# Two batch pairs through layer 3 with seven quarter products, and layer 0 of the first pair on two engines

## The chip, the core and the metric

The kernel runs on one core of a Trainium2 chip. The metric is the device time of one launch in microseconds. The core has a matrix engine (PE, which multiplies a stationary 128x128 operand with up to 512 moving columns into PSUM), a vector engine (DVE), an activation engine (ACT), GpSimd (POOL) and a queue engine (SP). All of them run their own instruction streams in order and meet through semaphores. Transfers between HBM and the on-chip memory are issued here by SP (loads of the adjacency matrix A) and by POOL (nearly everything else).

## What is computed

`x` is 8 x 2048 x 64, `adj` is a dense-stored 2048 x 2048 f32 matrix. Four layers follow each other; each adds its result to x and normalises over the 64 channels. Cut to what matters:

```python
# layer 0: Chebyshev stack, node-wise weights
x_g = [x, A @ x, 2 * A @ (A @ x) - x]                    # two products with A
out = einsum('bnki,nkio->bno', x_g, einsum('nd,dkio->nkio', embedding, weight)) + b
# layer 1: attention masked by adj > 0.5, softmax over nodes, elu
# layer 2: one product with A + I
agg = einsum('ij,bjh->bih', adj + eye, x @ W.T + b) / deg
# layer 3: three steps, one product with A each
for _ in range(3):
    effects = einsum('nm,bmd->bnd', adj, v)
    h = relu(concatenate([v, effects]) @ W1.T + b1)
    v = h @ W2.T + b2
x = layernorm(x + v)
```

## The kernel before

**Tiling.** The batch of 8 is worked on as four pairs; two batches of 64 channels fill the 128 rows of the array. A node vector of a pair is a [128, 16, 128] tile: nodes in 16 groups of 128, and 128 channels. `SX[p]` holds pair p, `SA`, `SB` and `SH` are further slots of that form. One product with A (`sweep`, L1040) runs over four column chunks of 512 nodes; each chunk accumulates 16 matmuls of 128x128 by 128x512, that is 64 per product. A comes as tiles [128, 2, 512] of 512 KB, two matmuls' worth, through a ring of seven buffers (`a_ring`, L219), which `fetch` (L223) fills in the order of `order_of_a`. All products are in full f32. In the profile each such matmul has two records.

**Stages.** `sweeps` (L1108) runs the products: the first product of pairs 0 and 1 on shared A tiles, then each pair's second product with the first one of a later pair, then for each pair in turn its layer 2 and its three steps of layer 3. In a step, `U = h W` is held for all nodes; the product's result goes through `h_evict` (L917, relu on ACT into `SH`), and `u_chunk` (L990) multiplies that chunk by a 128x128 block and writes the next U. `last_chunk` (L1010) and `store` (L1030) end a pair. The product of a step starts with a seed, one more 128x512 matmul per chunk for the part of W1 that acts on v (L1048).

Layer 0's node-wise weights are applied in `second_pass` (L553): for each tile of 128 nodes, two halves of 8 terms are multiplied into a PSUM buffer of two banks. `add_terms` (L590) drains a half by 8 ACT instructions, scaling by the embedding, into an SBUF tile `terms`; after the second half DVE adds up the 16 terms as a tree (L612). When all four buffers of that ring are taken, DVE drains with multiply-adds directly (L601). The PSUM buffers come from `pp_ring` (two of them), which also serves all transposes and small products. `po_ring` (one buffer) belongs to the attention product.

Layer 1 (`layer1`, L635, to `finish`, L828): `layer1` transposes x and makes the scores' two vectors; `scores` (L676) finds each row's greatest score on DVE with 32 instructions; `weights` (L773) makes the 16 x 2 blocks of attention weights, two DVE additions and two ACT passes each; PE multiplies them with x (L810); `finish` divides and normalises. When a pair is done, `at["x2", p]` is set, on which its layer 2 waits. The scores of a pair wait for those of the pair before. The mask by rows comes from `rows_of_adj` (L400), which loads adj row-wise, 1 MB per tile, at due times 115 + 13 t.

**What sets the order.** A planner, executed while the program is built, holds an estimated time for each engine and a set of generators ("threads"). Each thread says on which engine it wants to go on and after what; the thread that can begin first is emitted next, so each engine's stream is a merged, fixed order. The product sweeps have the lowest rank and fill PE when nothing else is ready. PE work that waits for something is planned with 2.5 us of slack. `tails` (L937) emits the small PE work behind each chunk in the order of the evictions.

Of the kernel before, what the change touches and what calls it, by code (L numbers as in the profile page):

```python
# [9 lines left out]
F32 = mybir.dt.float32  # L10
# [125 lines left out]
def resnorm_d4_kernel(  # L136
# [57 lines left out]
    def cols(c):  # L194
        return slice(c * CW, (c + 1) * CW)
# [24 lines left out]
    a_tiles = {}  # L220
    order_of_a = []

    def fetch(n):  # L223
        c, q, plus = order_of_a[n]
        t, k = a_ring.take([P, 2, CW], "a")
        freed = a_ring.t
        nc.sync.dma_start(
            t,
            a_plus_i[q]
            if plus and c == q // 2  # L230
            else adj_t[q * 2 * P : (q + 1) * 2 * P, cols(c)].rearrange("(t p) n -> p t n", p=P),
        )
        a_tiles[n] = (t, k)
        at["a", n] = plan.run("SP", 1.4, freed) + 3.5

# [91 lines left out]

    a_plus_i = [dram.tile([P, 2, CW], F32, name=f"a_plus_i{q}") for q in range(AQ)]

    y1_cols = [dram.tile([P, N], F32, name=f"y1_cols{p}") for p in range(NPAIR)]  # L330


# [67 lines left out]
    def rows_of_adj():  # L400


        for t in range(NT):
            yield "SP", [115.0 + 13.0 * t, bc_ring]
            an, k = bc_ring.take([P, 2, HALF], "an")
            an = an.rearrange("p a b -> p (a b)")
            nc.sync.dma_start(an, adj[t * P : (t + 1) * P, :])
            done = plan.run("SP", 2.8, bc_ring.t, 115.0 + 13.0 * t) + 9.0
            plan.start(1, row_tile(t, an, k, done))

    def row_tile(t, an, k, done):
# [141 lines left out]
    def second_pass():  # L553

        for n in range(NPAIR * NCH):
            yield "PE", [("y2", n + 1), ("xg", n + 1)]
            p, c, y2T, ky, got = queue[n]
            xg, kx = stacked[n]
            left = [TPC]
            for j in range(TPC):  # L560
                t = c * TPC + j
                cs = slice(j * P, (j + 1) * P)
                for h in range(2):
                    hs = slice(h * CW, (h + 1) * CW)
                    if h == 0 or pp_ring.ready() > plan.free["PE"]:
                        yield "PE", [("xg", n + 1), got, pp_ring]
                    if h == 0:


                        terms = None  # L570
                        if e_ring.ready() < NEVER:
                            terms = e_ring.take([P, D0, P], "terms")
                    yp, k = pp_ring.take([P, 2, CW], "yp")

                    for k2 in (h, 1 - h):
                        for e in range(2):
                            rows = slice(e * C, (e + 1) * C) if k2 else slice(0, P)
                            nc.tensor.matmul(  # L578
                                yp[:, e, :],
                                lhsT=y2T[rows, cs] if k2 else xg[:, e, cs],  # L580
                                rhs=(wk2 if k2 else w01)[rows, hs],
                                start=(k2 == h),
                                stop=(k2 != h),
                            )
                    t_pe = plan.run("PE", 2.8, got)
                    plan.start((2, 2, 1, 1)[p], add_terms(p, c, t, h, yp, k, terms, t_pe, left))
            yt_ring.give(ky, t_pe)
            xg_ring.give(kx, t_pe)

    def add_terms(p, c, t, h, yp, k, terms, t_pe, left):  # L590
        eng = "ACT" if terms else "DVE"
        yield eng, [t_pe]
        v = SX[p][:, t, :]
        for d in range(8):
            dd = h * 8 + d
            term = yp[:, :, d * C : (d + 1) * C]
            weight = emb_sb[:, t, dd : dd + 1]
            if terms:
                nc.scalar.activation(batches(terms[0][:, dd, :]), term, AF.Copy, scale=weight)  # L599
            else:  # L600
                nc.vector.scalar_tensor_tensor(  # L601
                    batches(v), term, weight, batches(v), ALU.mult, ALU.add
                )
        done = plan.run(eng, 8 * (0.25 if eng == "ACT" else 0.265), t_pe)
        pp_ring.give(k, done)
        if h == 0:
            return
        if terms:
            yield "DVE", [done]
            for half in (8, 4, 2):  # L610
                a, b = (terms[0][:, i * half : (i + 1) * half, :] for i in range(2))
                nc.vector.tensor_tensor(a, a, b, ALU.add)  # L612
            for d in range(2):
                nc.vector.tensor_tensor(v, v, terms[0][:, d, :], ALU.add)
            done = plan.run("DVE", 2.5, done)
            e_ring.give(terms[1], done)
        left[0] -= 1
        if left[0] == 0:
            plan.start(2, first_norm(p, c, plan.free["DVE"] + plan.LAG))
# [282 lines left out]

    def after_l2(p):
        return SB if p == 0 else SX[p - 1]

    def z_evict(p, c, pa, ka, done):
        yield "ACT", [done, yt_ring]
        z, kz = yt_ring.take([P, CW], "z")  # L910
        nc.scalar.copy(z, pa)
        done = plan.run("ACT", act(CW), done)
        acc_ring.give(ka, done)
        queue2.append(lambda: layer2_tail(p, c, z, kz, done))
        at["q2", len(queue2)] = done

    def h_evict(p, s, c, pa, ka, done):  # L917
        yield "ACT", [done]
        nc.scalar.activation(  # L919
            SH[:, tiles(c), :],  # L920
            pa.rearrange("p (t n) -> p t n", n=P),
            AF.Relu,
            bias=b31b if s == 0 else b31n,
        )
        done = plan.run("ACT", act(CW), done)
        acc_ring.give(ka, done)
        at["h", p, s, c] = done
        if s < 2:
            dst = SX[p] if s == 0 else SA
            queue2.append(lambda: u_chunk(p, c, ge, dst, ceb, s + 1, done))  # L930
        else:
            queue2.append(lambda: last_chunk(p, c, done))
        at["q2", len(queue2)] = done
# [33 lines left out]
    def start_chunk(p, c, v, done):  # L967

        done = yield from layer_norm(v, CW, done, True)
        if c == 0:  # L970
            v00 = tiny([P, P], "v00", 1)
            nc.vector.tensor_copy(v00, v[:, 0, :])
            nc.vector.tensor_copy(
                v00[0:1, :].rearrange("p (e c) -> p e c", c=C),
                ivc.unsqueeze(1).to_broadcast([1, 2, C]),
            )
            done = plan.run("DVE", dve(P, 2), done)
        yield "PE", [done, pp_ring]
        pt, k = pp_ring.take([P, TPC, P], "ps_vT")
        for j in range(TPC):  # L980
            nc.tensor.transpose(pt[:, j, :], v00 if c + j == 0 else v[:, j, :], ident)
        done = plan.run("PE", tr(TPC), done)
        eng = yield EITHER, [done]
        copy(eng, SH[:, tiles(c), :], pt)
        done = plan.run(eng, cost(eng, CW), done)
        pp_ring.give(k, done)
        at["h", p, -1, c] = done
        yield from u_chunk(p, c, w31e, SA, None, 0, done)

    def u_chunk(p, c, w, dst, bias, s, done):  # L990
        yield "PE", [done, pp_ring]
        pu, k = pp_ring.take([P, TPC, P], "ps_u")
        for j in range(TPC):
            nc.tensor.matmul(  # L994
                pu[:, j, :], lhsT=SH[:, c * TPC + j, :], rhs=w, start=True, stop=True
            )
        done = plan.run("PE", mm(P, TPC), done)
        if bias is None:
# [11 lines left out]
    def last_chunk(p, c, done):  # L1010
        yield "PE", [done, pp_ring]
        pv, k = pp_ring.take([P, TPC, P], "ps_v")
        for j in range(TPC):
            nc.tensor.matmul(  # L1014
                pv[:, j, :], lhsT=SH[:, c * TPC + j, :], rhs=w32c, start=True, stop=True
            )
        done = plan.run("PE", mm(P, TPC), done)
        at["spent", p, c] = done
# [62 lines left out]
    def refill():  # L1081
        while ahead[0] < len(order_of_a) and a_ring.ready() < NEVER:
# [2 lines left out]
            fetch(ahead[0])  # L1085
            ahead[0] += 1

    def first_product(p):
        return product(SX[p], lambda c, *a: y1_chunk(p, c, *a))

# [3 lines left out]
        )  # L1094

    def layer2_product(p):
        return product(SX[p], lambda c, *a: z_evict(p, c, *a), need=lambda q: [("x2", p)])

    def layer3_product(p, s):
        return product(  # L1100
            SX[p] if s == 1 else SA,
            lambda c, *a: h_evict(p, s, c, *a),
            need=lambda q: [("u", p, s, q)],
            before=lambda c: [("h", p, s - 1, c)],
# [3 lines left out]
    def sweeps():  # L1108

        order_of_a.extend((c, q, False) for _ in range(NPAIR) for c, q in sweep_of_a)  # L1110
        for p in range(NPAIR):
            for s in range(4):
                order_of_a.extend((c, q, s == 0) for c, q in sweep_of_a)
        refill()
        yield from sweep(first_product(0), first_product(1), masks=True)
        for p in range(NPAIR):
# [1 line left out]
            if 0 < p < NPAIR - 1:  # L1118
                products.append(first_product(p + 1))
            yield from sweep(*products)  # L1120
        for p in range(NPAIR):
            yield from sweep(layer2_product(p))
            for s in range(3):
                yield from sweep(layer3_product(p, s))


    ctx.enter_context(tc.manual_schedule())
# [47 lines left out]
```

## Time and profile before

| | |
|---|---|
| median of 3 runs | 2182.61 us (2180.09 to 2184.45) |
| profiled execution | 2179.89 us |
| its span, first to last instruction | 2178.1 us |
| granted PE clock | 0.993 |
| busy: PE, DVE, ACT, POOL | 2116.7, 1424.8, 973.0, 194.6 us |
| moved | 504.26 MB, mean 232 GB/s |
| A tiles loaded | 672 of 512 KB, 5.2 us to landing |
| layer 0 of pair 0 on PE | 151 to 311 us |
| first scores (pair 0) | 377.5 us |
| first layer-2 matmul of pair 2 | 1649.2 us |
| layer 1 of pair 3 done | 1707.6 us |
| last product ends, last store is issued | 2165.5, 2171.9 us |

A row of a timeline reads: start, duration, engine, line, operation, output<-inputs, shape, count; in brackets the idle time before it and what ended it. "xN" merges N instructions of a kind. The costliest groups of PE and ACT in layer 0, with busy time, mean ns of one and idle time before:

```profile
L578 PE MATMUL yp<-SH,xgT 128*128 128x512 f32 x512 | 249.9, 611 | 5.3 <-issue 2.1
L599 ACT ACTIVATE terms<-yp,emb_sb 128x128 f32<-128x128 f32 x928 | 251.8, 396 | 104.9 <-PE yp L578 104.8
```

Matmuls and ACT instructions are pipelined, so their mean durations overlap; a rate is read from a run of them, not from the mean.

### The profile page before, as it was taken

To read this page: it belongs to the slowest core of one execution; us is meant where nothing else is said; L and a number is where in the kernel's file an instruction comes from. 1 tells how busy PE (TensorE), PEld (TensorE's weight loads), DVE (VectorE), ACT (ScalarE), POOL (GpSimd) and SP (SyncE) were. 2 spreads that over 40 slices of the span, in tenths; PEclk is the share of its full clock that TensorE was granted. 3 is DMA by queue.
4 is the path that set the end of the run, shared out by engine and by line. 5 is a ranking of instruction groups with operands and counts; after the bars stand their busy time and mean duration, and the time that the engine had idled before them with its cause. 6 is when DMAs were issued, how large, how long until landed. Compare 5 with 4: busy or idle time off the path is not lost. (4 is left out here: it accounts for less than half of the span.)

```text
span 2178.1 us, 19094 instructions
## 1 busy us (share of the span) xinstructions
PE 2116.7 (97%) x6421; PEld 934.0 (43%) x6421; DVE 1424.8 (65%) x1823; ACT 973.0 (45%) x1761; POOL 194.6 (9%) x342
## 2 busy tenths in 40 slices
PE   8999999999999999999999999999999999999997
PEld 3444444433443333335443444444444544444443
DVE  2215554999789999989998989989797400121002
ACT  0016664467776555675724757417476200111001
POOL 2210000110011010000001011011010000000000
PEclk9999999999999999999999999999999999999999
DMA  9798764564344473347689778788787777887785
GB/s 312 270 323 297 241 201 146 165 208 123 113 159 122 132 245 110 121 129 258 214 304 345 237 274 297 255 307 292 241 270 226 247 263 269 282 289 247 265 277 182
DMA packets 228453, 504.26 MB, mean 232 GB/s; under 512 B 20530, under 2 KB 28850, under 8 KB 224242
## 3 DMA queue, kind: packets, MB, share of 16 engines
q1 hardware_dynamic: 189378, 372.79, 51.0%
q0 software_dynamic: 34752, 128.14, 17.4%
q10 hardware_dynamic: 4224, 2.10, 0.4%
q8 instruction: 51, 0.84, 0.2%
q14 instruction: 48, 0.39, 0.1%
HBM read 471.31 MB, written 29.56 MB: 230 GB/s over the span
## 5 line engine op out<-in xcount | busy, mean ns | idle before, releaser
L1059 PE MATMUL acc<-a,SX 128*128 128x512 f32 x1536 | 693.8, 597 | 9.4 <-DMA SX<-in_x 6.4
L1059 PE MATMUL acc<-a,SA 128*128 128x512 f32 x1280 | 575.0, 596 | 8.9 <-ACT SA L337 4.8
L1059 PEld LDWEIGHTS acc<-a,SX 128*128 128x128 f32 x1536 | 285.6, 191 | 350.7 <-issue 336.4
L1059 PEld LDWEIGHTS acc<-a,SA 128*128 128x128 f32 x1280 | 238.8, 191 | 293.9 <-issue 278.6
L792 ACT ACTIVATE e<-e,sv 128x1024 f32<-128x1024 f32 x256 | 280.9, 1153 | 108.8 <-DVE e L784 107.3
L706 DVE CUSTOM_DVE_ANT_0 junk<-s2b,mr 128x2048 bf16<-128x2048 f32 x128 | 292.8, 2287 | 24.3 <-DMA mr<-by_row 22.9
L800 ACT ACTIVATE e<-e 128x2048 f32<-128x2048 f32 x128 | 245.0, 1918 | 128.5 <-DVE e L797 128.0
L599 ACT ACTIVATE terms<-yp,emb_sb 128x128 f32<-128x128 f32 x928 | 251.8, 396 | 104.9 <-PE yp L578 104.8
L797 DVE TENSOR_TENSOR e<-e,mb 128x2048 f32<-128x2048 f32 x128 | 290.5, 2286 | 4.9 <-ACT e L792 4.7
L784 DVE TENSOR_TENSOR e<-s1b,mk 128x2048 f32<-128x2048 f32 x128 | 289.8, 2285 | 3.1 <-DMA mk<-by_col 3.1
L578 PE MATMUL yp<-SH,xgT 128*128 128x512 f32 x512 | 249.9, 611 | 5.3 <-issue 2.1
L810 PE MATMUL po<-e,SX 128*64 128x512 f32 x1024 | 236.4, 603 | 4.0 <-ACT e L800 4.0
L612 DVE TENSOR_TENSOR terms<-terms 128x1024 f32<-128x1024 f32 x174 | 135.7, 780 | 106.0 <-ACT terms L599 101.9
L578 PEld LDWEIGHTS yp<-SH,xgT 128*128 128x128 f32 x512 | 90.6, 190 | 149.9 <-issue 136.3
L578 PE MATMUL yp<-SH,y2T 64*128 64x512 f32 x512 | 131.3, 623 | 7.2 <-ACT terms L599 3.2
L810 PEld LDWEIGHTS po<-e,SX 128*64 128x64 f32 x1024 | 67.9, 137 | 160.1 <-issue 139.7
L1059 PE MATMUL acc<-a,SB 128*128 128x512 f32 x256 | 119.0, 594 | 0.0
L779 POOL DMA_DIRECT2D mk<-by_col x128 | 69.1, 541 | 537.7 <-DVE e L784 454.5
L919 ACT ACTIVATE SH<-acc,b31n 128x512 f32<-128x512 f32 x32 | 21.8, 681 | 209.8 <-PE acc L1059 209.8
L1003 DVE TENSOR_TENSOR SA<-ps_u,ceb 128x512 f32<-128x512 f32 x16 | 11.0, 689 | 118.5 <-PE ps_u L994 118.5
L1003 DVE TENSOR_TENSOR SX<-ps_u,ceb 128x512 f32<-128x512 f32 x16 | 11.0, 689 | 118.1 <-PE ps_u L994 118.1
L578 PEld LDWEIGHTS yp<-SH,y2T 64*128 64x128 f32 x512 | 42.9, 186 | 90.1 <-issue 78.7
(167 smaller groups left out, 1225.1 us busy)
## 6 DMA issues: line engine op xcount, KB each, us to landing
a<-in_adj_t SPq DMA_DIRECT2D x640, 512.0 KB, 5.2
mr<-by_row POOLq DMA_DIRECT2D x64, 512.0 KB, 5.7
mk<-by_col POOLq DMA_DIRECT2D x128, 256.0 KB, 5.2
an<-in_adj SPq DMA_DIRECT2D x16, 1024.0 KB, 8.7
a<-a_plus_i SPq DMA_DIRECT2D x32, 512.0 KB, 4.7
by_col<-mk POOLq DMA_DIRECT2D x32, 256.0 KB, 6.1
by_row<-mr POOLq DMA_DIRECT2D x16, 512.0 KB, 6.3
s2b<-s_rows POOLq DMA_DIRECT2D x8, 1024.0 KB, 7.3
```

The source lines that it names most:

```text
L578: nc.tensor.matmul(yp[:, e, :], lhsT=y2T[rows, cs] if k2 else xg[:, e, cs], rhs=(wk2 if k2 else w01)[rows, hs], start=(k2 == h), stop=(k2 ...
L599: nc.scalar.activation(batches(terms[0][:, dd, :]), term, AF.Copy, scale=weight)
L612: nc.vector.tensor_tensor(a, a, b, ALU.add)
L706: nc.vector.tensor_tensor_reduce(out=junk, in0=s2b[e][0], in1=masks[t][0], scale=1.0, scalar=LOWEST, op0=ALU.add, op1=ALU.max, accum_out=m ...
L779: nc.gpsimd.dma_start(mk, by_col[jt // 2][:, jt % 2, h * HALF : (h + 1) * HALF])
L784: nc.vector.tensor_tensor(e, s1b[0], mk.unsqueeze(1).to_broadcast([P, 2, HALF]), ALU.add)
L792: nc.scalar.activation(e[:, i, :], e[:, i, :], AF.Prelu, bias=sv[:, 2 + i, jt : jt + 1], alpha=ALPHA)
L797: nc.vector.tensor_tensor(e, e, mb[0], ALU.add)
L800: nc.scalar.activation(e, e, AF.Exp)
L810: nc.tensor.matmul(po[i * C : (i + 1) * C, f, :], lhsT=SX[p][:, t, i * C : (i + 1) * C], rhs=e[:, i, f * CW : (f + 1) * CW], start=(t == 0 ...
L1003: nc.vector.tensor_tensor(dst[:, tiles(c), :], pu, bias.unsqueeze(1).to_broadcast([P, TPC, P]), ALU.add)
L1059: nc.tensor.matmul(pa, lhsT=source[:, m, :], rhs=t[:, i, :], start=(m == 0 and not seed), stop=(m == NT - 1),)
```

## The change

Pairs 2 and 3 go through layers 2 and 3 together. Layer 2 stays an ordinary product, but the two pairs share each A tile (`joint_layer2`), in two halves of the chunks, so that the four tiles at the same place of A's four quarters are on chip at once. From these, DVE makes the four sums of quarters that Strassen's scheme (in Winograd's form) needs, and POOL's queue writes them to HBM (`sums`). Where A's diagonal was increased for layer 2, the unchanged tiles of the two diagonal quarters are loaded as well (`pure`). A step of layer 3 (`joint_layer3`) treats the U of both pairs as a 2x2 block matrix (node halves by pairs) and makes seven products of quarters, m1 to m7, with 2 x 8 matmuls each, 8 for each of the two column chunks k of a quarter. The stationary side is a quarter of U or a sum of quarters of U (`sums_of_u`), the moving side a quarter of A or one of its four sums. `combine` puts the results together through two SBUF tiles, u2 and u3. The joint part starts when layer 1 of pair 3 is done, as it takes over the ring of attention weights for its tiles.

In layer 0 of pair 0, `po_ring` serves as a third PSUM buffer, and while ACT drains the first half of a tile's terms, DVE drains the second by multiply-adds. The row-wise loads of adj are due at 115 + 9 t.

```diff
     def fetch(n):
         c, q, plus = order_of_a[n]
         t, k = a_ring.take([P, 2, CW], "a")
...
+        if isinstance(c, str):
+            src = sum_tiles[c][q]
+        else:
+            src = a_plus_i[q] if plus and c == q // 2 else tile_of_adj(c, q)
+        nc.sync.dma_start(t, src)
...
-            yield "SP", [115.0 + 13.0 * t, bc_ring]
+            yield "SP", [115.0 + 9.0 * t, bc_ring]
...
-                    if h == 0 or pp_ring.ready() > plan.free["PE"]:
-                        yield "PE", [("xg", n + 1), got, pp_ring]
+                    ring = pp_ring
+                    if p == 0 and po_ring.ready() < pp_ring.ready():
+                        ring = po_ring
+                    if h == 0 or ring.ready() > plan.free["PE"]:
+                        yield "PE", [("xg", n + 1), got, ring]
...
+        shared = p == 0 and terms is not None
+        eng = "ACT" if terms and not (shared and h) else "DVE"
...
         if terms:
-            yield "DVE", [done]
-            for half in (8, 4, 2):
+            yield "DVE", [done, ("terms", p, t)]
+            for half in (4, 2) if shared else (8, 4, 2):
...
+    JOINT = (NPAIR - 2, NPAIR - 1)
+    SH_of = {p: SH for p in range(NPAIR)}
...
+    def u_of(p, s):
+        return SX[p] if s == 1 else SB if p == NPAIR - 1 else SA
...
+    RQ = AQ // 2
+    def quarters(k, r):
+        return [(k, r), (k, r + RQ), (k + 2, r), (k + 2, r + RQ)]
+    def order_of_joint():
...
+        for s in range(3):
+            for m in ("a11", "a12", "s2", "s3", "a22", "s1", "s4"):
...
+    def pure(k, r):
+        yield "SP", [("group", k, r), *([xg_ring] if len(xg_ring.freed) > 1 else [NEVER])]
+        got = []
+        for c, q in (quarters(k, r)[i] for i in (0, 3)):
+            t, kt = xg_ring.take([P, 2, CW], "pure")
+            nc.sync.dma_start(t, tile_of_adj(c, q))
...
+    def sums(k, r, taken):
...
+        if r // 2 == k:
+            own = dict(zip((0, 3), (yield from pure(k, r))))
...
+        def out_of(m, a, b, op, *after):
+            yield "DVE", [bc_ring, *after]
+            t, kt = bc_ring.take([P, 2, HALF], m)
...
+            nc.vector.tensor_tensor(t, a, b, op)
+            done = plan.run("DVE", dve(2 * CW), *after)
+            nc.gpsimd.dma_start(sum_tiles[m][k, r], t)
...
+        s3, d3 = yield from out_of("s3", a11, a21, ALU.subtract, ready[0], ready[2])
+        s1, d1 = yield from out_of("s1", a21, a22, ALU.add, ready[2], ready[3])
+        s2, d2 = yield from out_of("s2", s1, a11, ALU.subtract, d1)
+        s4, d4 = yield from out_of("s4", a12, s2, ALU.subtract, d2)
+        for (_, kt, _, free), d in zip(taken, (d2, d4, d1, d1)):
+            a_ring.give(kt, max(free, d))
...
+    def joint_layer2():
...
+                    for e, pair in enumerate(JOINT):
+                        yield "PE", [("a", n)]
+                        t, kt = a_tiles[n]
+                        for b in range(2):
...
+                plan.start(5, sums(k, r, taken))
+                refill()
...
+    def joint_layer3():
...
+            for m, B, need, evict, seeded in (
+                ("m1", B11, u(p, 0), None, None),
+                ("m2", B21, u(p, 1), None, (p, 0)),
+                ("m6", T[1], t(1), "u2", None),
+                ("m7", T[2], t(2), "u3", None),
+                ("m4", T[3], t(3), "c21", (p, 1)),
+                ("m5", T[0], t(0), "c22", None),
+                ("m3", B22, u(o, 1), "c12", (o, 0)),
+            ):
+                for k in range(2):
...
+                    for r in range(RQ):
+                        n = next(used)
+                        yield "PE", [("a", n), need(r // 2)]
+                        at_, kt = a_tiles.pop(n)
+                        for b in range(2):
...
+                    if m == "m1":
+                        held[k] = (pa, ka)
+                        plan.start(1, keep_m1(s, k, pa, U, done))
+                    elif m == "m2":
+                        plan.start(1, h_evict(p, s, k, pa, ka, done))
+                    else:
+                        plan.start(1, combine(s, k, evict, pa, ka, U, done))
+                if m == "m4":
+                    for k in range(2):
+                        plan.start(1, seed_c22(s, k, seed, U))
+    def sums_of_u(s, T, B11, B21, B12, B22):
...
+            for i, a, b, after in (
+                (0, B12, B11, (u[2], u[0])),
+                (1, B22, T[0], (u[3], ("t", s, 0, k))),
+                (2, B22, B12, (u[3], u[2])),
+                (3, B21, T[1], (u[1], ("t", s, 1, k))),
+            ):
+                yield "DVE", after
+                nc.vector.tensor_tensor(T[i][:, ks, :], a[:, ks, :], b[:, ks, :], ALU.subtract)
...
+    def keep_m1(s, k, pa, U, done):
+        yield "ACT", [done]
+        nc.scalar.copy(U[:, 0, k * CW : (k + 1) * CW], pa)
...
+    def seed_c22(s, k, seed, U):
...
+        nc.tensor.matmul(pt, lhsT=seed, rhs=SH_of[o][:, tiles(2 + k), :], start=True, stop=True)
...
+        nc.vector.tensor_tensor(u3, u3, pt, ALU.add)
...
+    def combine(s, k, what, pa, ka, U, done):
...
+        if what in ("u2", "u3"):
+            yield "DVE", [done]
+            nc.vector.tensor_tensor(u2 if what == "u2" else u3, u2, pa, ALU.add)
...
+        nc.vector.tensor_tensor(tmp, u2 if what == "c12" else u3, pa, ALU.add)
...
+        if what == "c22":
+            nc.vector.tensor_tensor(u2, u2, pa, ALU.add)
...
+        pair, half = {"c21": (p, 1), "c22": (o, 1), "c12": (o, 0)}[what]
+        yield from h_evict(pair, s, 2 * half + k, tmp, None, done)
...
-        for p in range(NPAIR):
+        for p in range(NPAIR - 2):
             yield from sweep(layer2_product(p))
             for s in range(3):
                 yield from sweep(layer3_product(p, s))
+        yield "PE", [("x2", NPAIR - 1)]
+        h_o, _ = e_ring.take([P, 2, HALF], "h_o")
+        SH_of[NPAIR - 1] = h_o.rearrange("p a (t n) -> p (a t) n", n=P)
+        yield from joint_layer2()
+        yield from joint_layer3()
```

## The prediction

> **What bounds the kernel now.** I read the page's 40 slices first, then PE by stages, then the timelines around the two places that the change touches.
>
> ```profile
> PE   8999999999999999999999999999999999999997
> DVE  2215554999789999989998989989797400121002
> ```
>
> TensorE is full from end to end. VectorE is full from slice 7 to slice 30 (380 to about 1680 us) and nearly idle after that. So two engines are co-critical for 1300 us, and the last 470 us belong to PE alone. PE's busy share could be stretched, so I check its rate in the chain of waits:
>
> ```profile
> 1439.70 0.86 PE acc L1048 x2
> 1444.99 10.30 PE acc L1059 x24
> ```
>
> A 128x512 f32 matmul is two records; 24 records in 10.30 us are 0.858 us per matmul. In stages (windows; PE, PEld, DVE, ACT, POOL busy, clock, DMA share, GB/s):
>
> ```profile
> 0.00:1655.00 1655.00, 1607.75 (x4948) 687.69 (x4949) 1327.12 (x1606) 909.64 (x1647) 187.31 (x332) 0.99 0.67 224
> 1655.00:1708.00 53.00, 53.00 (x177) 25.12 (x176) 36.24 (x70) 20.81 (x30) 1.29 (x2) 1.00 0.71 230
> 1708.00:2165.00 457.00, 454.30 (x1292) 220.27 (x1290) 58.70 (x141) 40.85 (x82) 5.27 (x7) 1.00 0.78 265
> 1143.50:1197.90 54.40, 50.30 (x149) 21.62 (x148) 45.38 (x35) 24.90 (x24) 9.31 (x17) 1.00 0.95 345
> ```
>
> PE idles 47 us before 1655 and under 3 in the whole late stage. The fourth row is the densest DMA window: 345 GB/s, share 0.95, PE 4 us short. Where pair 3 ends layer 1 (timelines of PE and DVE):
>
> ```profile
> 1649.17 1.88 PE L1059 MATMUL acc<-a,SX 128*128 128x512 f32 x4
> 1673.17 3.65 PE L810 MATMUL po<-e,SX 128*64 128x512 f32 x16
> 1677.75 7.03 PE L1059 MATMUL acc<-a,SX 128*128 128x512 f32 x16
> 1684.62 1.05 PE L845 MATMUL pf<-back,poT 128*128 128x130 f32 x8
> 1706.89 0.69 DVE L487 TENSOR_TENSOR SX<-SX,ln_r 128x512 f32<-128x512 f32 x1
> ```
>
> Pair 2's layer 2 starts at 1649 as filler; pair 3's last attention product ends at 1676.8; its normalised x is ready at 1707.6. Up to then PE has done 96 records, 48 matmuls, of pair 2's layer 2.
>
> **The joint steps, PE work.** Each of three steps has 7 products of 2x8 matmuls, 112, in place of 2x64 = 128: 48 fewer, 48 x 0.858 = 41.2 us. Nothing else falls: seeds stay 8 a step (m2, m4, m3 two each, seed_c22 two), chunk matmuls are the same, and layer 2 stays 128. Two pairs' work before is 512 + 24 seeds at 0.858, 24 chunk products ps_u and 16 of ps_emb and ps_v at 0.89, 8 transposes at 0.44: 499 us. After: 458.
>
> **The new wait.** The joint part waits for pair 3's x. Behind that wait on PE stands all that is left, and nothing else is there to fill: the 48 matmuls (41.2 us) and 3 us of small pieces done before 1707.6 now come after it. If that moment stays, this alone eats the 41 us. A little comes free: with no filler, pf follows the last attention product at once rather than at 1684.62 (7.8 us, of which the poT copy takes 1.2), and two layer-2 tails leave DVE. I take 6 us: 1701.6.
>
> **Is that moment earlier?** That is the work of the other half. In layer 0 of pair 0 (151 to 311 us on PE) a tile has 5.4 us of matmuls, but tiles come every 9 us:
>
> ```profile
> 160.16 1.88 PE L578 MATMUL yp<-SH,xgT 128*128 128x512 f32 x4
> 165.70 3.60 PE L1059 MATMUL acc<-a,SA 128*128 128x512 f32 x8
> 169.14 1.88 PE L578 MATMUL yp<-SH,xgT 128*128 128x512 f32 x4
> ```
>
> Two PSUM buffers must be drained by ACT (2.18 us per half) before the next tile, and 3.4 us of product fill the gap. These 160 us are 16 x 5.4 = 86 of tiles, 36 of pair 0's own second product, 27.5 of other pairs' products (32 matmuls) and 10 of small pieces and gaps. With a third buffer (the idle po) and DVE draining every second half, tiles run back to back, and pair 0 needs only its own product: the 27.5 us go behind it, less about 8 while the last y2 chunk is awaited. Gain 20 us. The half on DVE costs 8 x 0.27 = 2.2 us (the row of L601: 33.7 us over 96) against 1.22 saved in the add tree: 16 us in all, where DVE is 15 to 57% busy, so hidden. The closer pace of row loads (1 MB every 9 us, not 13) puts 16 SP loads, 16 ACT passes of 2.2 us and POOL writes earlier; SP's A fetches queue behind them. From 130 to 151 us the trace has DMA share 0.97 and PE 1.5 us short; bounds 0 and 6 us, I take 2.
>
> Then pair 0's scores:
>
> ```profile
> 338.02 0.60 PE L647 MATMUL ps_xT<-ident,SX 128*128 128x128 f32 x4
> 349.16 0.95 PE L657 MATMUL ps_sv<-a,xT 128*128 128x4 f32 x8
> 360.75 0.27 PE L759 MATMUL ps_rows<-ident,sv 128*64 128x128 f32 x1
> ```
>
> From the norm (324.8) to the first score (377.5) pass 52.7 us, for three tiny PE steps 11 us apart: pair 1's tiles hold the two pp buffers. After the change pair 1's y2 comes about 20 us later relative to pair 0, so the buffers are mostly free. Bounds 0 and 25 us; I take 12. Head start: 20 + 12 - 2 = 30 us.
>
> Does it last until 1677? From 377.5 to 1677 DVE is busy 1195.7 of 1299.5 us, its waits are short, and PE's 27.5 us of postponed filler come back only where it has slack: pair 2's and 3's layer 0 are normed at about 830 and 990, their scores begin at 1035 and 1312. I take 0.9 of it, 27 us: x of pair 3 at 1701.6 - 27 = 1675. **PE's own bound**: busy up to 1707.6 is 1607.75 + 52.6, less 44 postponed = 1616; with all 47 us of idle it is 1663. So PE would wait some 12 us, and the joint part starts at 1676.
>
> **Costs inside the joint part.** DVE: four sums of 128x1024 at 1.22 (row L612) are 4.9 us per group of 16 matmuls (13.7 us); in a step 26 operations of 0.69, 18 us in 110. DVE is busy 58.7 of 457 us there, so PE covers them; without cover it would be 39 us for the sums. But the A slots now wait for these sums and for the "pure" loads, which stand in SP's queue behind fetches for the next group.
>
> Transfers in joint layer 2: 32 tiles read, 8 pure, 32 sums written by POOL's queue, 72 x 0.524 = 37.7 MB in about 115 us: 328 GB/s. The groups with pure loads (two in a row at the start, two at the end) move 5.24 MB in 13.7 us, 382 GB/s. Here a rule speaks against the change: the Trainium skill's page DMA: Bandwidth & Descriptors, in Specifications, puts the HBM limit of one core at about 358 GB/s. By it two such groups take 29.3 us, 1.8 more than PE; by the 345 GB/s window 30.4, 2.9 more. I take the row. Seven prefetched tiles cover the first two groups, so 3 us; bounds 0 and 10.
>
> Entering step 0: pair 2's chunk 1 ends 8.6 us before the last layer-2 matmul; from z to u a chunk takes 15.8 us alone (1724.1 to 1739.9), and m1 asks for it 3.4 us in: 4 us late, of which other chunks' PE pieces cover half. I take 3; bounds 0 and 10. Later steps ask late enough: m6, the first to need all of U, stands 32 matmuls (27 us) into a step. The two such entries of before (1.35 us each) go: -3. The end is now 12.7 us after the last product; the combine adds 0.7 and a neighbour's norm on DVE some: 14.
>
> ```profile
> 2155.08 10.46 PE L1059 MATMUL acc<-a,SA 128*128 128x512 f32 x24
> 2171.90 0.75 POOL L1032 DMA_DIRECT2D out<-SX  x1 [11.49 <-DVE SX L487]
> ```
>
> **Sum.** 1676 + 457 (458 less the last ps_v, in the tail) + 3 + 3 - 3 + 3 for small misorders = 2139, + 14 = 2153 us of span. The profiled execution of before took 1.8 more than its span and the median of the runs 2.7 more than that: 2157.5, so **2157**, 1.2% faster.
>
> **Rivals.**
> 1. The head start is lost on the way (pair 1's layer 0 lacks the postponed PE work, or DVE finds new waits). Joint start 1702, span 2179, runs 2183: no change. For it: PE never idles from 163 to 270 us, so all of pair 1's layer 0 is PE-paced; against: DVE still holds 147 us of pair 0's weights then.
> 2. It becomes slower: joint layer 2 is held by its transfers. The place is the A ring, released only after sums whose writes pass through four bc slots and POOL's queue (6.3 us landing for 512 KB before). The price is 37.7 MB over the rate, less 115 us: at 240 GB/s, near the mean of 232, 42 us, so 2157 + 39 = 2196. It decides below about 260 GB/s (30 us lost). Against: the 345 window.
> 3. More is won: pair 0's scores start 45 us earlier and PE's idle time of 47 us halves, since PE has postponed work in hand. Start 1645, span 2122, runs 2127. For it: the waits of 11 us on pp; against: PE's idle pieces are spread waits of an in-order queue.
>
> **Chances.** Forecast 0.65 (its own range 2138 to 2176), rival 1 0.13, rival 2 0.10, rival 3 0.12. What tells a change of this kernel from none is about 0.2%, 4.4 us. Faster: 0.64 + 0.12 + 0.04 of rival 1 = 0.80; same: mostly rival 1, 0.07; slower: 0.10 + 0.03 = 0.13. The range 2130 to 2186 leaves out half of rival 3 and most of rival 2.
>
> **What would show it.** First scores (L706 of before) at about 345 us instead of 377; tiles of pair 0 about 6 us apart; pair 3's x near 1675 with PE idle some 12 us before the joint part; 928 records (464 matmuls) in the products of the last two pairs, against 1024; last product about 460 us after its start; PE busy 41 us less. It is wrong if pair 3's x stays near 1700, if PE waits for A tiles by more than 10 us in joint layer 2, or if a step takes over 115 us.

## The result, and the profile after

The changed kernel takes 2172.5 us (median of 5 runs, 2172.0 to 2177.3), against 2182.6 before: ratio 0.9957, 95% interval 0.9940 to 0.9973. That is 10 us faster, where 25.6 were forecast. The range (2130 to 2186) holds it and the sign is right; the size is not.

The profiled execution took 2177.3 us, the slowest of the five, with a span of 2175.5 us and a granted clock of 0.984 (before: 0.993). That of the kernel before took 2179.9, 2.7 us under its median, so the two profiles lie 2.6 us apart where the medians lie 10: some of what the changed kernel's profile shows as late belongs to this one execution. From the page of the changed kernel, the busy times and the 40 slices:

```profile
PE 2090.3 (96%) x6325; PEld 923.0 (42%) x6325; DVE 1532.3 (70%) x2057; ACT 933.5 (43%) x1605; POOL 213.3 (10%) x374
PE   8998999999999999999998999989999998999997
DVE  2226756999799999979998978989797555020214
```

PE was to be busy 41 us less; it is 26 us less (2116.7 before), and its idle time rose from 61 to 85 us. DVE's slices 3, 4 and 6, counted from 0, are fuller by the second halves that it now drains, and the 5s of slices 31 to 33 hold the four sums. The stages of the changed kernel (windows; PE, PEld, DVE, ACT, POOL busy, clock, DMA share, GB/s), and the same first stage of the kernel before:

```profile
0.00:1632.00 1632.00, 1569.92 (x4802) 671.33 (x4803) 1326.87 (x1717) 842.85 (x1460) 184.62 (x325) 0.99 0.66 219
1632.00:1688.00 56.00, 55.93 (x195) 23.78 (x194) 41.62 (x35) 37.67 (x35) 4.75 (x8) 1.00 0.72 227
1688.00:1818.00 130.00, 126.63 (x371) 62.09 (x369) 69.98 (x127) 16.73 (x39) 16.27 (x30) 0.99 0.75 267
1818.00:1848.00 30.00, 21.66 (x85) 14.25 (x84) 18.28 (x43) 8.40 (x20) 1.60 (x3) 0.83 0.76 234
1848.00:2163.00 315.00, 314.96 (x871) 150.55 (x869) 69.61 (x124) 25.64 (x46) 4.54 (x6) 1.00 0.80 263
```

```profile
0.00:1632.00 1632.00, 1584.75 (x4873) 678.33 (x4873) 1304.78 (x1590) 890.65 (x1630) 184.90 (x328) 0.99 0.67 224
217.60:380.00 162.40, 161.45 (x478) 69.61 (x477) 82.83 (x169) 93.57 (x289) 11.63 (x21) 1.00 0.58 198
1380.00:1480.00 100.00, 91.56 (x266) 44.45 (x265) 88.42 (x112) 26.75 (x39) 12.46 (x23) 0.97 0.87 305
```

Ahead of 1632 us PE is idle for 62 us where it was idle for 47, and it has made fewer matmuls by then. From 1632 to the joint part it is full: PE does not wait for pair 3 there; it has work left. The last two rows of the kernel before are read further on.

Layer 0 of pair 0 does run back to back, then stalls (timeline of PE, changed kernel):

```profile
155.05 3.70 PE L593 MATMUL yp<-SH,xgT 128*128 128x512 f32 x8
158.68 1.99 PE L593 MATMUL yp<-SH,y2T 64*128 64x512 f32 x8
160.59 3.70 PE L593 MATMUL yp<-SH,xgT 128*128 128x512 f32 x8
...
176.84 1.98 PE L593 MATMUL yp<-SH,xgT 128*128 128x512 f32 x4
...
195.61 1.13 PE L593 MATMUL yp<-SH,y2T 64*128 64x512 f32 x4
202.48 2.08 PE L593 MATMUL yp<-SH,y2T 64*128 64x512 f32 x4 [5.75 <-ACT terms L616]
204.49 2.90 PE L593 MATMUL yp<-SH,xgT 128*128 128x512 f32 x4
```

After a wait of 5.75 us eight instructions of the kinds that took 1.13 and 1.98 us before take 2.08 and 2.90; the granted clock from 202.5 to 206.5 us is 0.52. ACT had come late because it stood behind DVE, and DVE behind the write of a mask row (timelines of DVE and ACT, same kernel; the brackets are the chain):

```profile
186.58 1.23 DVE L431 TENSOR_SCALAR mr<-an 128x2048 bf16<-128x2048 f32 x1 [10.11 <-DMA by_row<-mr]
195.62 0.63 ACT L480 ACTIVATE ln_sq<-SX 128x512 f32<-128x512 f32 x1 [12.30 <-DVE SX L473]
```

The first scores begin at 351.4 us, where 377.5 was before. Layer 1 ends in four blocks a pair, each begun by one division in `finish`. Pair 0's come 20 to 41 us earlier than before; those of pair 1 from 16 us earlier to 2.5 later; those of pair 2 0.4 to 10 us later; the last of pair 3 (1696.9 us) when it did before. The joint part starts at 1688 us:

```profile
1687.15 1.13 PE L863 MATMUL pf<-back,poT 128*128 128x130 f32 x8
1688.12 5.31 PE L1205 MATMUL po<-a,SX 128*128 128x512 f32 x12
1696.81 2.65 PE L1205 MATMUL po<-a,SX 128*128 128x512 f32 x4 [3.37 <-DVE SX L498]
...
1818.34 1.05 PE L974 MATMUL ps_emb<-w2bd,z 128*128 128x128 f32 x8
1826.20 2.32 PE L1008 MATMUL ps_vT<-ident,SX 128*128 128x128 f32 x8 [6.81 <-DVE SX L498]
1829.96 2.08 PE L1021 MATMUL ps_u<-w31e,SH 128*128 128x128 f32 x8 [1.44 <-ACT SH L348]
...
2161.08 1.88 PE L1292 MATMUL acc<-a,SB 128*128 128x512 f32 x4
2164.50 1.16 PE L1041 MATMUL ps_v<-w32c,h_o 128*128 128x128 f32 x8 [1.53 <-ACT h_o L946]
```

It starts on x that is not complete: pair 3's x is ready at 1705.4 us, 2.2 us earlier than before and not 33, so one of the prediction's own signs of being wrong ("if pair 3's x stays near 1700") came true. In the plan the joint part starts when layer 1 of pair 3 is done; on the chip its products begin as soon as the first tiles are there. PE waits 3.4 us for a tile within layer 2, 6.8 and 1.4 us on the way into step 0, and never again until the last product ends at 2163.0; the products are 928 records, as forecast. At the entry DVE is the one that is late: a norm of pair 2's chunk stands there behind the sums T of the next step (L1327) and behind sums of A (L1165):

```profile
1811.65 0.69 DVE L1327 TENSOR_TENSOR t<-SB,SA 128x512 f32<-128x512 f32 x1
1813.90 1.22 DVE L1165 TENSOR_TENSOR s<-pure,a 128x1024 f32<-128x1024 f32 x1 [1.56 <-issue]
1815.04 0.68 DVE L1327 TENSOR_TENSOR t<-SB,t 128x512 f32<-128x512 f32 x1
...
1821.96 1.22 DVE L1165 TENSOR_TENSOR s<-a,pure 128x1024 f32<-128x1024 f32 x1
...
1825.46 0.69 DVE L498 TENSOR_TENSOR SX<-SX,ln_r 128x512 f32<-128x512 f32 x1
```

### The profile page after: what moved, and what is told of

The parts are those of the page before. It is cut to its first block, busy times and chain, and to the rows that moved or that the text cites. A ratio compares the mean times of both kernels' runs of the same rounds, so it can differ in the third digit from the quotient of the medians.

```text
span 2175.5 us, 19004 instructions
## 1 busy us (share of the span) xinstructions
PE 2090.3 (96%) x6325; PEld 923.0 (42%) x6325; DVE 1532.3 (70%) x2057; ACT 933.5 (43%) x1605; POOL 213.3 (10%) x374
## 5 line engine op out<-in xcount | busy, mean ns | idle before, releaser
L1086 PE MATMUL acc<-a,SX 128*128 128x512 f32 x1024 | 470.1, 603 | 9.0 <-DMA SX<-in_x 6.4
L1086 PE MATMUL acc<-a,SA 128*128 128x512 f32 x768 | 352.9, 602 | 8.0 <-ACT SA L348 4.7
L1086 PEld LDWEIGHTS acc<-a,SX 128*128 128x128 f32 x1024 | 191.7, 193 | 242.7 <-issue 229.1
L616 ACT ACTIVATE terms<-yp,emb_sb 128x128 f32<-128x128 f32 x768 | 207.9, 396 | 70.9 <-PE yp L593 70.6
L1086 PEld LDWEIGHTS acc<-a,SA 128*128 128x128 f32 x768 | 142.6, 192 | 182.0 <-issue 168.3
L1292 PE MATMUL acc<-a,t 128*128 128x512 f32 x384 | 169.1, 592 | 0.0
L630 DVE TENSOR_TENSOR terms<-terms 128x512 f32<-128x512 f32 (+1 forms) x152 | 111.2, 731 | 35.6 <-ACT terms L616 32.2
L618 DVE SCALAR_TENSOR_TENSOR SX<-yp,emb_sb,SX 128x128 f32<-128x128 f32 x256 | 89.7, 350 | 48.9 <-PE yp L593 40.4
L1292 PEld LDWEIGHTS acc<-a,t 128*128 128x128 f32 x384 | 72.0, 190 | 86.1 <-issue 86.1
L480 ACT ACTIVATE ln_sq<-SX 128x512 f32<-128x512 f32 x48 | 30.4, 633 | 146.4 <-DVE SX L473 81.1
```

The costliest lines, as they stand in the source:

```text
L618: nc.vector.scalar_tensor_tensor(batches(v), term, weight, batches(v), ALU.mult, ALU.add)
L1086: nc.tensor.matmul(pa, lhsT=source[:, m, :], rhs=t[:, i, :], start=(m == 0 and not seed), stop=(m == NT - 1),)
L1292: nc.tensor.matmul(pa, lhsT=B[:, 2 * r + b, :], rhs=at_[:, b, :], start=(r == 0 and b == 0 and not go_on), stop=(r == RQ - 1 and b == 1), ...
```

## Experiments

Three parts of the change can be undone singly: the joint steps, the sharing of layer 0 (with its third buffer), and the pace of the row loads. The first four runs take parts away; later ones fill the corners. Medians in us; before is 2182 to 2184 in each comparison:

| | rows 13 us | rows 9 us |
|---|---|---|
| neither | 2182.6 (before) | 2202.7 |
| sharing | 2187.9 | 2198.4 |
| joint steps | 2169.4 | 2175.5 |
| both | 2162.0 | 2172.5 (the change) |

**Joint steps alone, rows 13.**

```diff
-                    if p == 0 and po_ring.ready() < pp_ring.ready():
+                    if p < 0 and po_ring.ready() < pp_ring.ready():
...
-        shared = p == 0 and terms is not None
+        shared = p < 0 and terms is not None
...
-            yield "SP", [115.0 + 9.0 * t, bc_ring]
+            yield "SP", [115.0 + 13.0 * t, bc_ring]
...
```

> Joint steps alone; layer 0 of pair 0 and the pace of the row loads (13 t) as before. Theory 1 (PE is full until the joint part and sets its start, so a head start of the attention chain is worth nothing): PE fills up to about 1663 + 10, joint start at about 1680 or earlier, time 2160 to 2172, not slower than the changed kernel. Theory 2 (the attention chain of pair 3 sets the start and the head start was needed to bring it forward): x of pair 3 at 1701 as the prediction had it without a head start, PE idle 30 us or more before the joint part, time 2184 to 2190.

2169.4 us (2167.4 to 2172.5), ratio 0.9940 (0.9928 to 0.9953). Here PE does wait for pair 3. Its timeline:

```profile
1659.87 5.06 PE L828 MATMUL po<-e,SX 128*64 128x512 f32 x16 [2.72 <-ACT e L818]
1672.33 5.65 PE L828 MATMUL po<-e,SX 128*64 128x512 f32 x16 [7.41 <-ACT e L818]
1679.10 2.05 PE L863 MATMUL pf<-back,poT 128*128 128x130 f32 x16 [1.12 <-ACT poT L348]
1680.99 5.31 PE L1205 MATMUL po<-a,SX 128*128 128x512 f32 x12
1689.12 2.90 PE L1205 MATMUL po<-a,SX 128*128 128x512 f32 x4 [2.81 <-DVE SX L498]
```

The filler is gone and the attention weights arrive one by one, as the prediction's new wait said: 13.6 us of PE's time between 1632 and 1688 are idle, and what follows a gap is slow (5.06 and 5.65 us for the 16 instructions that take 3.65, at a granted clock of 0.72 and 0.64). But the joint part begins at 1681.0, where the prediction had 1701.6 without a head start: it needs only the first tiles, and not x as a whole (1697.7).

**Sharing alone, rows 9** (layer 3 of all pairs as before).

```diff
-        for p in range(NPAIR - 2):
+        for p in range(NPAIR):
...
-        yield from joint_layer2()
-        yield from joint_layer3()
...
```

> Layer 0 of pair 0 on two engines and rows at 9 t alone; all of layer 3 as before. Theory 1: PE's work is unchanged and its stalls grow as in the changed kernel (idle plus 15 us, slow clock plus 10 before 1688), so slower than before: 2190 to 2205. Theory 2: the head start has nothing to bring forward here but costs nothing: 2180 to 2185.

2198.4 us (2197.4 to 2206.0), ratio 1.0082 (1.0068 to 1.0096). First scores at 346.8 us, 31 us ahead of before, and the kernel is 16.6 us slower. The lead is there, and the loss is the pace's: against the kernel before at the same pace (2202.7 us, below) the sharing saves 4.3 us.

**The change with rows at 13 us.** The edit is the one above, on the two lines with the pace.

> The changed kernel with the row loads back at 13 t. If the closer pace is what stalls VectorE on the by_row stores at 176 to 186 us and through ACT holds PE at 196 to 202 us (5.75 us of idle and 4 us at half clock), the time falls by 5 to 12 us to 2160 to 2167 under theory 1. Theory 2: the rows are needed early for the first scores, which then move from 351 back towards 377, and the time rises to 2175 to 2190.

2162.0 us (2160.4 to 2164.5), ratio 0.9909 (0.9893 to 0.9924): 10.5 us better than the change. First scores 341.1 us, the stall at 197 us gone, joint start 1671.9. So the closer pace, priced at 2 us, cost ten, and made the first scores later. PE's stages ahead of the joint part in this run:

```profile
0.00:1632.00 1632.00, 1578.96 (x4860) 674.20 (x4861) 1348.48 (x1745) 848.83 (x1445) 185.70 (x329) 0.99 0.66 222
1632.00:1672.00 40.00, 39.92 (x139) 17.73 (x138) 26.02 (x26) 23.11 (x23) 2.59 (x4) 1.00 0.70 219
```

With the sharing PE does not wait for pair 3, where joint steps alone, at the same pace, left it idle for 13.6 us. Ahead of 1632 us it is idle for 53 us, 9 less than in the change, and 6.0 of these 9 lie between 163 and 220 us, at the stall.

**The change with late sums.** The first of the four sums T waits until the first product of the step is through.

```diff
-                (0, B12, B11, (u[2], u[0])),
+                (0, B12, B11, (u[2], u[0], ("m1", s, 1))),
```

> The changed kernel with the sums of U held back until m1 is kept. If the entry to step 0 (8.3 us of PE idle at 1818 to 1832 and half clock after it) comes from VectorE's order, where the sums of U for k=0 stand before pair 2's norm, 2.7 us of DVE work leave that chain: PE idle there falls by 3 to 6 us, time 2166 to 2170. If the chunk's own chain of z, norm and U sets it, nothing changes: 2172.

2167.7 us (2167.1 to 2168.9), ratio 0.9932 (0.9920 to 0.9945): 4.8 us better than the change. The 8.25 us of idle at the entry become 3.96:

```profile
1815.44 0.66 PE L1008 MATMUL ps_vT<-ident,SX 128*128 128x128 f32 x4 [2.07 <-DVE SX L498]
1817.99 2.07 PE L1021 MATMUL ps_u<-w31e,SH 128*128 128x128 f32 x8 [1.89 <-ACT SH L348]
```

**Both mends** (rows at 13 us and late sums).

> The changed kernel with the reads of the degree rows paced at 13 us a tile, as before the change, and with the sums T of the second step waiting for the product of step 0, as in the two kernels run singly. Theory 1 (the two losses lie in different stages, both on the engine that sets the end): their gains add, 2162.0 - 4.9 = 2157, first scores near 341, joint part from near 1672, TensorE idle in the 30 us before step 0 near 4. Theory 2 (what is won at the entry is only taken from a wait further on): 2162.

2156.3 us (2154.3 to 2157.3), ratio 0.9881 (0.9867 to 0.9894). The two gains add, and the time is that of the forecast, 2157. Its PE at the entry to step 0:

```profile
1805.66 0.66 PE L1008 MATMUL ps_vT<-ident,SX 128*128 128x128 f32 x4 [0.58 <-DVE SX L498]
1808.21 1.16 PE L1021 MATMUL ps_u<-w31e,SH 128*128 128x128 f32 x8 [1.89 <-ACT SH L348]
1810.21 1.12 PE L1008 MATMUL ps_vT<-ident,SX 128*128 128x128 f32 x4 [0.84 <-DVE SX L498]
```

**Sharing alone, rows 13.** Both edits: that of the sharing alone, and the pace.

> The sharing of layer 0 alone, layer 3 of all four pairs as before, and the degree rows at 13 us a tile. If the row pace is what made the sharing alone 16.6 us slower than the kernel before: near the time before or under it, 2174 to 2184 (first scores near 338, 163 to 217 us without idle). If the sharing itself costs time further on (the scores of pairs 1 and 2, which came 13 and 65 us apart from before), the row pace is worth its 10 us and no more: 2186 to 2192.

2187.9 us (2186.7 to 2192.0), ratio 1.0025 (1.0014 to 1.0036): the second branch. Without the stall the sharing by itself still costs 5.6 us. Under the joint steps, at the same pace, it wins 7.4 (2169.4 to 2162.0): there it takes PE's wait for pair 3 away.

**The kernel before with rows at 9 us.**

> The kernel before with nothing changed but the pace of the degree rows, 9 us a tile for 13. If the pace by itself makes VectorE wait for a row and TensorE behind it: 2188 to 2193. If it costs only together with the sharing, whose tiles need VectorE sooner: 2181 to 2184, with no idle of TensorE over 1 us in 163 to 217 that the kernel before does not have.

2202.7 us (2200.9 to 2204.2), ratio 1.0091 (1.0076 to 1.0107). Both branches miss: one number in the program costs 20 us, twice what the first branch allowed, and not where either looked. Between 163 and 380 us PE is idle 1.8 us (before: 1.0). Of the 18.6 us by which its idle time ahead of 1632 us grows, 8.0 lie a thousand microseconds behind the rows, in layer 2 of pair 1, and 7.3 between 380 and 600 us (windows of this run, then its waits of PE from 1380 to 1480 us; the same wait took 5.2 us in the kernel before):

```profile
0.00:1632.00 1632.00, 1566.14 (x4802) 670.01 (x4803) 1305.70 (x1607) 875.93 (x1587) 182.91 (x325) 0.99 0.65 220
1380.00:1480.00 100.00, 83.65 (x256) 40.11 (x255) 89.23 (x115) 25.38 (x40) 11.34 (x21) 0.91 0.78 273
```

```profile
PE ps_vT L981 <- DVE SX L487: 10.7, 3, 10.2
```

The row loads end long before. What reaches so far is the order that the planner writes: a due time that moves lets another thread go first. With 9, 11 and 15 us alike, PE's instructions leave the order of the kernel before at 189 us, and DVE's between 176 and 186 us, in layer 0 of pair 0. In the order of this run, the norm for which PE waits 10.2 us stands in DVE's queue behind two instructions of the scores, 2.28 us each.

**Second groups first.** Both mends, and in the second half of the joint layer 2 the row groups in the order 2, 3, 0, 1, so that the last one has no `pure` tiles to wait for.

```diff
+    def rows_of(k):
+        return [(r + k * RQ // 2) % RQ for r in range(RQ)]
...
-            for r in range(RQ):
+            for g, r in enumerate(rows_of(k)):
```

> As the kernel with both mends (13 us rows, late T), and in the second half of the joint layer 2 the row groups in the order 2, 3, 0, 1, so that the last group has no second load of A to wait for when its sums are made. If VectorE's queue at the entry to step 0 is held by that load: idle of TensorE before step 0 from 4 down to 1 to 2 us, 2153 to 2155. If the 4 us that are left are the chain of the last chunk's norm, no gain: 2157, and a loss of 2 to 4 us if the two groups with second loads now come too early for the queue that fetches them.

2156.1 us (2151.8 to 2159.4), ratio 0.9880 (0.9866 to 0.9893): no gain over the two mends. The waits at the entry stay (0.2, 1.9 and 0.9 us), so it is not the second loads that make them. That leaves the chain from z to U, which no run took apart.

**Joint steps alone, rows 9.**

> The joint steps alone as in the run of them alone, but with the degree rows at 9 us a tile: the corner that is missing among joint, sharing and pace. If the joint steps are worth 26 us wherever TensorE has no idle time ahead of them (as with the sharing, at 13 and at 9 us rows; the kernel before with rows at 9 has none in the 54 us ahead of layer 3): 2202.7 - 26 = 2177. If they are worth 13 us wherever layer 0 is not shared, since pair 3's attention ends too late for their start: 2190.

2175.5 us (2172.0 to 2181.9), ratio 0.9967 (0.9954 to 0.9981): the first branch. Against the changed kernel this run differs in the sharing alone; its first scores begin at 377.8 us, 26 us later than the change's, and its joint part at 1687.1 us, 1 us earlier (a window of PE's stages, then the timeline):

```profile
1632.00:1687.00 55.00, 54.92 (x194) 23.36 (x193) 40.69 (x35) 36.76 (x35) 4.21 (x7) 1.00 0.69 224
...
1687.08 5.31 PE L1205 MATMUL po<-a,SX 128*128 128x512 f32 x12
```

PE is full from 1632 us to the joint part here too, so there is no wait for pair 3 that a lead could shorten. How far this one pair of traces can be trusted shows in the run with late sums: the order of its instructions is that of the change up to the joint part, and it gets there at 1682.1 us, with first scores at 348.8. So a lead of 26 to 29 us is worth between -1 and 5 us at the joint start, and 3.0 us in the medians.

**Other paces**, to see whether a fast pace is the cost or any other order.

```diff
-            yield "SP", [115.0 + 13.0 * t, bc_ring]
+            yield "SP", [115.0 + 11.0 * t, bc_ring]
```

> The kernel before with the degree rows at 11 us a tile. If the pace costs by itself, the faster the more (9 us: 20.4 us): between, 2188 to 2196. If each pace only makes the planner write another order of the whole kernel, with another set of waits: anything from 2180 to 2203, with no order by pace; the waits of TensorE then lie far behind the rows, at the norm of layer 2 (1380 to 1480 us) and not at 115 to 320 us.

> The kernel before with the degree rows at 15 us a tile. If a fast pace costs by itself, a slower one costs nothing: 2178 to 2184. If each pace only draws another order: slower than 13 by some 5 to 20 us, 2187 to 2202, as long as 13 is the best of its neighbours.

> The changed kernel with the rows at 15 us a tile and the late sums T. If a fast pace costs by itself: as with 13, 2154 to 2158. If each pace only draws another order: anywhere from 2150 to 2168, and which pace is best here need not be the one that is best in the kernel before.

At 11 us the kernel before takes 2202.0 us (ratio 1.0084, 1.0070 to 1.0098), at 15 us 2211.7 (1.0127, 1.0114 to 1.0141), beyond what either theory gave. The changed kernel with late sums and 15 us takes 2175.0 (0.9958, 0.9946 to 0.9970), seven above the upper end; with 9 and 13 it took 2167.7 and 2156.3. There is no order by pace: 9, 11, 13, 15 give +20, +18, 0, +28 us in the kernel before. The loss goes with idle time of PE ahead of 1632 us in each case, here that of 15 and, below it, of the sharing alone at 13:

```profile
0.00:1632.00 1632.00, 1562.89 (x4772) 669.31 (x4773) 1287.73 (x1574) 879.59 (x1614) 182.38 (x323) 0.98 0.65 218
```

```profile
0.00:1632.00 1632.00, 1581.34 (x4863) 675.72 (x4864) 1349.13 (x1745) 849.47 (x1445) 185.38 (x329) 0.99 0.66 222
```

Idle 69 and 51 us there, 66 at 9 us and 64 at 11, 47 before; times +28, +6, +20, +18. Which single decision of the planner is the costly one was not tried.

## Why the prediction was wrong in size

**The steps that failed.** Two terms of the sum hold the 15.5 us that are missing. The row pace, "bounds 0 and 6 us, I take 2", cost 10.5 us; the entry to step 0, "I take 3; bounds 0 and 10", was 8.25 us of idle time, and holding one sum back wins 4.8 us of the kernel's time. Without the two the kernel takes 2156.3 us, for 2157 forecast. That this is so near is in part luck, since two larger errors cancel in it: the new wait and the head start.

**The new wait** was put at 1701.6 us without a head start; joint steps alone begin at 1681.0. That the joint part must wait for all of pair 3's x was wrong: it begins on the first tiles.

**The head start**, "I take 0.9 of it, 27 us", is there at its origin (first scores at 351, with rows at 13 even 341, forecast 345). It can be worth no more at the joint start than the wait of PE for pair 3 that it takes away. That wait is 13.6 us in the joint steps alone with rows at 13, and there 38 us of lead are worth 9 at that start and 7.4 in the time. With rows at 9 there is no such wait, and 26 us of lead are worth 3.0 in the time. For the rest, PE is busy 161.45 of 162.40 us between 218 and 380 in the kernel before: it was not short of work while pair 0's scores were late, and to bring pair 0's tiles forward moved other products behind them. Ahead of an unchanged layer 3 the sharing costs 5.6 us at rows of 13 and saves 4.3 at rows of 9 (2202.7 to 2198.4), as each edit writes another order too; so a few of these microseconds cannot be put down to the lead itself. The first rival had named the loss on the way, but with a joint start at 1702, which was as wrong as the new wait.

The drain by DVE was misread as well: the row of L601 gives 33.7 / 96 = 0.35 us an instruction, not 0.27, and eight take 3.05 us in the changed kernel, not 2.2. From 150 to 320 us PE waits for these drains by 0.3 us in all, so this decided little.

**PE's bound, 1663, was 1672 with rows at 13 us and 1688 in the change's profile.** The forecast kept the idle time of the kernel before, 47 us, as if it were a property of the stages. It belongs to the order. With rows at 13, PE's busy time to the joint start is 1619 us for a forecast of 1616, and its idle time 53. The change has 62 us idle and 1626 busy, the latter with the slow instructions behind the stall. Together +25, of which the joint start shows +12, since 1676 had been put above the bound; six of them may belong to this execution, as the run with late sums got there at 1682.1 in the same order.

**The row pace** cost 10.5 us with the rest of the change and 20.4 us by itself. The prediction counted its loads, passes and writes and left out that every due time is an input of the planner. In the change a stall of 5.75 us, within the bounds, is the direct part; in the kernel before the loss lies behind it, in other waits. Which decision of the planner makes them stays open.

**The entry to step 0**: the prediction named the chain from z to u and not the competitors in DVE's queue; late sums take 4.3 us of idle time off it, and 3.3 are left with both mends. The granted clock from 1826.2 to 1834.0 us is 0.50. From joint start to last product it is 475 us for a forecast of 463; with both mends 469.

**The transfers**: the second rival, a joint layer 2 held by its transfers, did not come. The DMA slices of the joint layer 2 of the changed kernel (40 slices of 3.25 us):

```profile
DMA  8320008999559999992899075699999980899964
GB/s 283 124 83 0 0 0 243 354 399 396 221 178 266 390 416 413 412 408 107 236 305 400 27 234 226 100 370 409 412 338 420 408 291 25 231 355 398 399 234 166
```

Between slices that stand nearly still it moves 390 to 420 GB/s, for up to five slices on end. The limit of about 358 GB/s that the prediction took from the Trainium skill's DMA: Bandwidth & Descriptors (Specifications), and the 345 of the window, both lie below what this stretch reaches; the measurement decides, and the forecast's 3 us for such groups should have been nothing: no wait of PE for an A tile shows in this stretch.

**The tail**: forecast 14, measured 12.5 us from the last product to the end of the span.

**The sum.** Span 2153 + 12 (joint start) + 12 (joint part) - 1.5 (tail) = 2175.5, the measured one. The median of the runs is 4.8 us below that profiled execution, where the forecast had put it 2.7 above its own, so 15.5 us separate the two figures.

The version with both mends, 2156.3 us, is faster than both kernels, by 26 us than before and by 16 than the change.

## What to carry to other kernels

Before a head start is priced, look at the engine that sets the end in the stretch where the late work is waited for: the head start is worth at most the wait that it takes away there. If that engine is full, it only changes the order of the work, and the price is what the new order does to its idle time. In a kernel whose order is merged by a planner, a due time is an edit of the whole program: one number cost 18 to 28 us here, some of it a thousand microseconds behind its place, so try each such number by itself, and again after every other edit. A sum that is wanted late should not be put into a queue early.

## What the chip showed that was not expected

Small gaps cost PE more than their length. In the changed kernel, in layer 2 of pair 1:

```profile
1438.18 0.63 PE L1008 MATMUL ps_vT<-ident,SX 128*128 128x128 f32 x4 [1.47 <-DVE SX L498]
1440.76 1.16 PE L1021 MATMUL ps_u<-w31e,SH 128*128 128x128 f32 x8 [1.95 <-ACT SH L348]
1443.79 6.18 PE L1086 MATMUL acc<-a,SA 128*128 128x512 f32 x8 [1.88 <-ACT SA L348]
...
1450.78 3.60 PE L1086 MATMUL acc<-a,SA 128*128 128x512 f32 x8
```

Eight records take 6.18 us after three waits of 1.5 to 2 us each, 5.3 us in all within 7.1, and 3.60 a few microseconds later; the granted clock is 0.60 from 1443.8 to 1450.0 us and 1.00 in the 5 us after that. The Trainium skill's TensorE: Matmul & The Clock Gate (Part 1: The HAM clock gate) has the array at half rate after an idle window of about 3.4 us, until it has been busy for as long. The single gap of 5.75 us in layer 0 agrees with it (clock 0.52 behind it, 1.9 us lost on eight records). None of the gaps shown here is as long by itself; several short ones with little work between them were enough, at 2.6 us. In all, 18.6 us more idle time in the kernel before with rows at 9 us made its span 24.4 us longer, 16.8 with rows at 11 us 20.1, and 21.8 with rows at 15 us 34.2: an idle microsecond of PE went with 1.2 to 1.6 us of span.
